# A graph network in two layers: the scan of layer 1 into SBUF, register loads of layer 2 in other places, and more columns fetched on chip

## The chip, the core and the metric

The kernel runs on one core of a Trainium2 chip. The core has five engines with a queue each: TensorE (PE in the profile, its weight loads PEld), VectorE (DVE), ScalarE (ACT), GpSimd (POOL) and SyncE (SP). They run side by side and meet at semaphores. Each queue is worked off in its order; some of its instructions, register loads for example, are done by the queue itself (DVEq and ACTq in the profile) and not by the engine behind it. The metric is device time in microseconds (us) of one execution, lower is better. Before the change it is 3579.78 us (median of 3 runs, 3579.74 to 3582.63).

## The reference

12500 nodes with 128 features and 200000 edges, sorted by destination (`dst`):

```python
h = maximum(layernorm(x), 0)
w = edge_weight / maximum(segment_sum(edge_weight, dst), EPS)[dst]
feat = relu(h @ W_pool + b_pool)
neigh = segment_max(feat[src] * w[:, None], dst)          # layer 1: a maximum per node
rst = h @ W1_self + neigh @ W1_neigh + b1
h = relu(rst / maximum(norm(rst), EPS))
neigh2 = segment_sum(h[src] * w[:, None], dst) / maximum(deg, 1)   # layer 2: a mean per node
out = x + relu(h @ W2_self + neigh2 @ W2_neigh + b2)
```

## The kernel before

Edges are worked in groups of 512, 391 groups, each of four chunks of 128 edges. A preparation computes `feat` and writes it to HBM (`feat_d`); then layer 1 runs over the groups, and layer 2 over them again. The order on each queue is the order in which the program is written out (a manual schedule), so a turn `i` of a loop issues different stages of several groups.

**Gathers and columns.** The rows `feat[src]` (layer 1) and `h[src]` (layer 2) of a chunk come by one indirect DMA from POOL (`gather`, line 520), 128 rows at a time, into a ring of buffers. Both tables also lie in SBUF with nodes as columns (`one_way`, `other_way`). For some groups one chunk is therefore not gathered: the class `Columns` copies its 128 columns out of the table, and PE turns them round. There are two such streams. Stream 0 runs on DVE and takes chunk 1: `two_by_two` (line 792) copies two columns by one instruction, 64 for a chunk. Stream 1 runs on ACT and takes chunk 3 in layer 1 and chunk 2 in layer 2: `one_by_one` copies one column by one instruction (line 780), 128 for a chunk. Which groups are taken is `first + int(n * every)`; `every` is 6 and 5.5 in layer 1, 3 and 3.5 in layer 2.

A column's place is known only at run time: a list of 128 places is brought to SBUF (`load`, on SP), and `places_of` loads 16 of them into registers of the engine's queue with one register load (line 742). A fetch is a burst of 16 columns with the registers loaded before; eight bursts make a chunk, spread over the turns ahead of its use (`plan`). `ahead` issues the register load for the next burst. With `ahead_of` false (both streams of layer 2, ACT's of layer 1) it is issued directly behind each burst; with `ahead_of` true (DVE's of layer 1) it waits for the call of `ahead` behind the scan, except between two bursts of one turn.

**Layer 1, a turn.** POOL gathers for group i. ACT scales the four chunks by the edge weights into `gs` (line 1027, two buffers). PE transposes `gs` into PSUM, `pm` (line 1032). DVE runs the segmented maximum along the edges with one scan, in place in PSUM (line 1047), with a mask `kt` that SP brings in from HBM for four groups at a time (`keep_rows`, `KEPT`). Then DVE copies the last column of the scan as `carry` (line 1066), copies every second column into `sc` (line 1070) and replaces some of these by their neighbours (`copy_predicated`, line 1073). PE transposes `sc` (line 1087), ACT copies the result to SBUF (`rows`, line 1042), and a product with a 0/1 matrix `sel` picks the last edge of each node. For column groups PE multiplies the columns by `W_pool`, and ACT applies the relu (`cut`, line 946). Besides, node tiles, and `side_step`s that prepare tables for layer 2, run in between. The first 16 groups take another way (rows of `x` gathered and multiplied).

**Layer 2, a turn.** DVE makes `hit` (line 1157) and from it the weighted places `s` (line 1160); between the two stands one burst of columns. PE multiplies the gathered rows by `s` into `pa` (line 1168). DVE adds the window of an earlier group to the sums (`window_add`, line 1171). The columns' chunks are turned round by PE into `flip` (`turned`, line 1143), and ACT copies them into the ring (`back`). At the end of the turn come the other bursts of both streams. Every fourth turn or so an output tile is finished (lines 902 and 903, DVE). The ring has eight buffers: POOL can gather into one when PE has used what it held.

## Time and profile before

| what | value |
|---|---|
| median of 3 runs | 3579.78 us |
| the profiled execution | 3579.99 us |
| its span in the trace | 3578.2 us |
| layer 1: first and last scan with a carry (line 1047) | 131.9 and 1843.1 us |
| layer 2: first and last gather of `h_d` into the ring | 1857.6 and 3546.9 us |
| gathers in layer 1 into `gt`, in layer 2 | 1192, 1318 |
| register loads of line 742: DVE, ACT | 1480, 1392 |
| granted TensorE clock, mean | 0.528 |

A row of a group of instructions reads: line, engine, operation, out<-in with shapes, count | busy us, mean ns of one | idle time of the engine in front of them and what ended it. Busy time is a union: instructions of one engine overlap, so busy divided by count can be less than the mean duration. Register loads, semaphores and the issue of DMAs are not counted as busy. In a row of waits stand the waiting engine and line, the one it waited for, then us in total, how often, and the longest. "issue" means that no other engine's event ended the wait.

### The profile page before, as it was taken

The numbers are of one execution on the slowest core, as the hardware profiler recorded it, in microseconds if no ns is written. First come the engines' busy times: TensorE is split into PE (matmuls) and PEld (weight loads), VectorE is DVE, ScalarE is ACT, GpSimd is POOL, SyncE is SP. The second block draws the span as 40 slices with busy tenths as digits, with TensorE's granted clock in tenths as the row PEclk, the third lists the DMA queues.
The fourth block names the chain that finished last, engine by engine and source line by source line (L and its number), as shares of the span: only waits on it lengthen the run. The fifth ranks groups of instructions, "written<-read, shape, count | busy, mean of one in ns | idle before, by whom it ended". The sixth has DMA issues, their size and how long they took to land.

```text
span 3578.2 us, 71950 instructions
## 1 busy us (share of the span) xinstructions
PE 2210.3 (62%) x9504; PEld 1929.0 (54%) x9504; DVE 3130.7 (87%) x16737; ACT 3087.4 (86%) x25633; POOL 2616.9 (73%) x2784
## 2 busy tenths in 40 slices
PE   7666666666766666566656666555655565555556
PEld 6455655565655555555545555544544454455445
DVE  7799999999999999998866888888888888888886
ACT  6689999999999998998948888888888888888885
POOL 6577777777777777777777777777777777777774
PEclk7665555555555555555555555555555555555555
DMA  6433222222222222222221122222222222222221
GB/s 222 130 95 95 87 88 83 87 87 87 91 88 87 86 88 86 86 87 82 86 78 54 54 66 69 62 60 63 58 60 58 61 57 61 60 59 57 60 62 46
DMA packets 132987, 280.13 MB, mean 78 GB/s; under 512 B 49446, under 2 KB 58764, under 8 KB 132494
## 3 DMA queue, kind: packets, MB, share of 16 engines
q0 software_dynamic: 88544, 181.42, 17.9%
q1 hardware_dynamic: 43214, 93.11, 7.5%
q14 instruction: 414, 3.39, 0.3%
q8 instruction: 79, 1.29, 0.2%
q10 hardware_dynamic: 736, 0.92, 0.1%
HBM read 253.41 MB, written 21.87 MB: 77 GB/s over the span
## 4 chain that ended last, share of the span: by engine, by line
DVE 42%; ACT 20%; issue 12%; DMA 7%; PE 7%; POOL 6%; DVEq 5%; ACTq 1%; POOLq 0%
DVE gt L792 22%; ACT gt L780 9%; POOL gt L520 6%; ACT gs L1027 6%; DVE pm L1047 4%; DVEq L742 4%; DVE picked L792 4%; DMA gt<-feat_d,srcT 4%; DMA gt<-h_d,srcT 3%; PE pa L1168 3%; DVE place L1157 2%; DVE sel L1059 2%; DVE way L1171 2%; PE pf L625 2%; DVE s L1160 1%
## 5 line engine op out<-in xcount | busy, mean ns | idle before, releaser
L780 ACT ACTIVATE gt<-way 128x1 f32 x21376 | 2123.3, 189 | 105.5 <-PE pa L1168 62.5
L520 POOL DMA_INDIRECT gt<-h_d,srcT x1318 | 1244.6, 944 | 446.3 <-issue 322.4
L520 POOL DMA_INDIRECT gt<-feat_d,srcT x1192 | 1126.7, 945 | 369.6 <-issue 271.5
L792 DVE SCALAR_TENSOR_TENSOR gt<-b,way 128x2 f32<-128x2 f32 x8000 | 1145.6, 214 | 64.9 <-issue 55.4
L1168 PE MATMUL pa<-s,gt 128*128 128x24 f32 x3102 | 736.7, 390 | 570.9 <-DVE s L1160 503.4
L1168 PEld LDWEIGHTS pa<-s,gt 128*128 128x128 f32 x3102 | 690.7, 328 | 608.5 <-DVE s L1160 533.4
L1032 PE MATMUL pm<-ident,gs 128*128 128x128 f32 x1499 | 398.9, 419 | 254.5 <-ACT gs L1027 230.6
L792 DVE SCALAR_TENSOR_TENSOR picked<-b,way 128x2 f32<-128x2 f32 x3840 | 542.0, 211 | 2.1 <-issue 1.8
L1047 DVE TENSOR_TENSOR_SCAN pm<-kt,carry,pm 128x512 f32<-128x512 bf16 x389 | 496.2, 1275 | 43.9 <-PE pm L1032 43.6
L1027 ACT ACTIVATE gs<-gt,ewT 128x128 f32<-128x128 f32 x1303 | 414.9, 390 | 73.2 <-DMA gt<-feat_d,srcT 59.4
L1096 PEld LDWEIGHTS pn<-sel,rows 128*128 128x128 f32 x1564 | 358.1, 316 | 164.7 <-ACT way L977 68.0
L1032 PEld LDWEIGHTS pm<-ident,gs 128*128 128x128 f32 x1499 | 288.2, 224 | 291.0 <-ACT gs L1027 266.6
L1096 PE MATMUL pn<-sel,rows 128*128 128x48 f32 x1564 | 360.4, 377 | 129.5 <-ACT way L977 53.5
L1059 DVE TENSOR_SCALAR sel<-cols,lastT,invT 128x48 f32<-128x48 f32 x782 | 244.1, 312 | 0.2 <-issue 0.2
L1087 PE MATMUL pr<-ident,sc 128*128 128x128 f32 x782 | 237.4, 405 | 3.5 <-DVE r_first L291 2.5
L1157 DVE TENSOR_TENSOR place<-place,locT 128x96 f32<-128x96 f32 x391 | 103.9, 266 | 108.9 <-DVE gt L792 80.5
L1160 DVE TENSOR_TENSOR s<-place,w2T 128x96 f32<-128x96 f32 x391 | 100.6, 257 | 82.0 <-DVE gt L792 67.4
L1087 PEld LDWEIGHTS pr<-ident,sc 128*128 128x128 f32 x782 | 165.5, 221 | 4.4 <-ACT gs L1027 3.8
L1073 DVE COPY_PREDICATED sc<-kt,pm 128x256 f32<-128x256 int16 x389 | 167.1, 429 | 0.0
L1070 DVE COPY sc<-pm 128x256 f32<-128x256 f32 x391 | 159.6, 408 | 4.0 <-PE pr L1087 3.9
L780 ACT ACTIVATE gt<-flip 128x128 f32<-128x128 f32 x108 | 29.6, 274 | 145.7 <-PE flip L1143 142.7
L1042 ACT ACTIVATE rows<-pr 128x256 f32<-128x256 f32 x392 | 141.8, 362 | 5.0 <-PE pn L1096 5.0
(303 smaller groups left out, 2774.9 us busy)
## 6 DMA issues: line engine op xcount, KB each, us to landing
kt<-keep_d SPq DMA_DIRECT2D x97, 512.0 KB
gt<-h_d,srcT POOLq DMA_INDIRECT x1318
gt<-feat_d,srcT POOLq DMA_INDIRECT x1192
feat_d<-fr SPq DMA_DIRECT2D x24, 256.0 KB
xr<-in_x SPq DMA_DIRECT2D x24, 256.0 KB
out<-o SPq DMA_DIRECT2D x24, 256.0 KB
h_d<-h SPq DMA_DIRECT2D x47, 128.0 KB
listed<-at_d SPq DMA_DIRECT2D x359, 0.5 KB
```

What stands on the lines that cost most here:

```text
L520: nc.gpsimd.indirect_dma_start(out=gt[:k, j, :], out_offset=None, in_=table_d[:, :], in_offset=bass.IndirectOffsetOnAxis(ap=srcT[:k, t, j, ...
L780: nc.scalar.activation(out, in_, AF.Copy, **scale)
L792: nc.vector.scalar_tensor_tensor(slot[:, r + e:r + e + 2], zero_high, columns_read[e], columns_read[e + 1].to_broadcast([P, 2]), op0=OP.su ...
L1027: nc.scalar.activation(gss[i][:k, j, :], gt[:k, j, :], AF.Copy, scale=ewT[:k, t, j, r:r + 1])
L1032: nc.tensor.transpose(pms[i - 1][:, j * P:j * P + k], gs[:k, j, :], ident[:k, :k])
L1047: nc.vector.tensor_tensor_scan(pm[:, :ne], kt[:, :ne], pm[:, :ne], carry, op0=OP.add, op1=OP.max)
L1059: nc.vector.tensor_scalar(part, cols[:k, 1, :], lastT[:k, t, j, r:r + 1], invT[:k, t, j, r:r + 1], op0=OP.is_equal, op1=OP.mult)
L1073: nc.vector.copy_predicated(sc[:, :ne // 2], new[:, :, 1], two[:, :, 0])
L1087: nc.tensor.transpose(prs[g][:k, j, :], sc[:, j * P:j * P + k], ident)
L1096: nc.tensor.matmul(pas[g], rows[:k, j, :], sel[:k, j, :], start=j == 0, stop=j == len(chunks) - 1)
L1157: nc.vector.tensor_tensor(hit, iota, locT[:, t, :, r:r + 1].to_broadcast([P, Q, CW]), OP.is_equal)
L1168: nc.tensor.matmul(pas[g][:, SHIFT[j]:SHIFT[j] + CW], gt[:k, j, :], s[:k, j, :], start=False, stop=j == 0)
```

## The change

- **Layer 1, scan.** The scan writes into the `gs` buffer of its group, in SBUF, in place of PSUM; `gs` has four buffers in place of two. The copy of every second column into `sc` is gone for all but the first 16 groups: `copy_predicated` works in place on every second column, and PE transposes those. `carry` is copied from SBUF. In the first 16 turns one product stands earlier.
- **Layer 1, mask.** It comes for three groups at a time, and the load is issued at the end of the turn.
- **Layer 1, columns.** `every` is 5 and 5.25.
- **Layer 2, register loads.** `ahead_of` is `None`: nothing is loaded directly behind a burst of DVE's. `ahead` is called behind `hit`, behind `s` and behind the window addition; a second burst stands ahead of the window addition; ACT's bursts stand around `back`, with `ahead` behind each of the later ones; `back` stands ahead of `turned`.
- **Layer 2, columns.** `every` is 2.85 and 3.3.

```diff
-KEPT = 4
+KEPT = 3
...
         def fetch(self, g, r):
+            if self.pending:
+                self.ahead()
             if (g, r) not in self.held:
                 self.places_of(g, r)
...
                     self.pending = g2, r2
-                    if not self.ahead_of or turn == self.order[now][2]:
+                    if self.ahead_of is False or self.ahead_of and turn == self.order[now][2]:
                         self.ahead()
...
+        def fetch_rest(self, i):
+            for step, g, r in self.plan.get(i, ()):
+                if step == self.fetch:
+                    step(g, r)
+                    self.ahead()
...
-                (0, mybir.EngineType.DVE, two_by_two, 1, 6, FIRST + 16),
-                (1, mybir.EngineType.Activation, one_by_one, 3, 5.5, FIRST + 12)):
+                (0, mybir.EngineType.DVE, two_by_two, 1, 5, FIRST + 16),
+                (1, mybir.EngineType.Activation, one_by_one, 3, 5.25, FIRST + 12)):
...
-            if i % KEPT == 0 and i and i + 2 < NG:
-                keep_rows(i + 2, keep_tile())
             if FIRST <= i < NG:
                 gts[i] = gather(buffer(i, True), feat_d, i, besides=bycol)
...
-                gss[i] = wk.tile([P, G], F32, name="gs", bufs=2).rearrange("p (q d) -> p q d", d=D)
+                gss[i] = wk.tile([P, G], F32, name="gs", bufs=4).rearrange("p (q d) -> p q d", d=D)
...
-                gs = gss.pop(i - 1)
+                gs = gss[i - 1]
...
-                nc.vector.tensor_tensor_scan(pm[:, :ne], kt[:, :ne], pm[:, :ne], carry,
+                most = gss.pop(g).rearrange("p q d -> p (q d)") if g >= FIRST else pm
+                nc.vector.tensor_tensor_scan(most[:, :ne], kt[:, :ne], pm[:, :ne], carry,
                                              op0=OP.add, op1=OP.max)
...
-                    nc.vector.tensor_copy(carry, pm[:, ne - 1:ne])
-                sc = scs[g] = wk.tile([P, G // 2], F32, name="sc", bufs=2)
-                two = pm[:, :ne].rearrange("p (c two) -> p c two", two=2)
-                new = kt[:, :ne].bitcast(I16).rearrange("p (c two) -> p c two", two=2)
-                nc.vector.tensor_copy(sc[:, :ne // 2], two[:, :, 1])
-            pick()
-            if g is not None:
-                nc.vector.copy_predicated(sc[:, :ne // 2], new[:, :, 1], two[:, :, 0])
+                    nc.vector.tensor_copy(carry, most[:, ne - 1:ne])
...
+            if g is not None:
+                two = most[:, :ne].rearrange("p (c two) -> p c two", two=2)
+                new = kt[:, :ne].bitcast(I16).rearrange("p (c two) -> p c two", two=2)
+                scs[g] = two[:, :, 1]
+                if g < FIRST:
+                    scs[g] = wk.tile([P, G], F32, name="gs", bufs=4)[:, :ne // 2]
+                    nc.vector.tensor_copy(scs[g], two[:, :, 1])
+            pick()
+            if g is not None:
+                nc.vector.copy_predicated(scs[g], new[:, :, 1], two[:, :, 0])
...
+            if i % KEPT == 0 and i and i + 2 < NG:
+                keep_rows(i + 2, keep_tile())
...
-                (0, mybir.EngineType.DVE, two_by_two, 1, 3, 17),
-                (1, mybir.EngineType.Activation, one_by_one, 2, 3.5, 12)):
+                (0, mybir.EngineType.DVE, two_by_two, 1, 2.85, 17),
+                (1, mybir.EngineType.Activation, one_by_one, 2, 3.3, 12)):
...
-            bycol.append(Columns(engine, copy, False, other_way, 1, lists_of(k), slot,
+            bycol.append(Columns(engine, copy, None, other_way, 1, lists_of(k), slot,
...
             nc.vector.tensor_tensor(hit, iota, locT[:, t, :, r:r + 1].to_broadcast([P, Q, CW]), OP.is_equal)
             if between:
+                bycol[0].ahead()
                 between()
...
                 weighted_places(i, lambda: bycol[0].fetch_one(i))
+                bycol[0].ahead()
...
+            by_two, by_one = bycol
+            by_two.fetch_one(i)
             g = i - 2
             if EARLY <= g < NG:
                 window_add(g, window_at(mybir.EngineType.DVE, g))
+            by_two.ahead()
+            by_two.turn(i, by_two.fetch)
+            by_one.fetch_one(i)
+            for c in bycol:
+                c.turn(i, c.back)
             for c in bycol:
                 c.turn(i, c.turned)
-                c.turn(i, c.back)
-            for c in bycol:
-                c.turn(i, c.fetch)
+            by_one.ahead()
+            by_one.fetch_rest(i)
```

More of the change, by code (lines that the diff above doesn't have):

```diff
@@ L1013, in gnn_kernel @@
                 if i + 1 < FIRST:
-                    weight_rows(i + 1, wk.tile([P, G], F32, name="gs", bufs=2))
+                    weight_rows(i + 1, wk.tile([P, G], F32, name="gs", bufs=4))
                     raw_columns(pn, i + 1)
```

## The prediction

> **What bounds the kernel now.** I read the first page, then the busy times by stretch, then each engine's waits inside a stretch, and last the instructions in order of time where the waits named no other engine.
>
> ```profile
> span 3578.2 us, 71950 instructions
> PE 2210.3 (62%) x9504; PEld 1929.0 (54%) x9504; DVE 3130.7 (87%) x16737; ACT 3087.4 (86%) x25633; POOL 2616.9 (73%) x2784
> DVE 42%; ACT 20%; issue 12%; DMA 7%; PE 7%; POOL 6%; DVEq 5%; ACTq 1%; POOLq 0%
> ...
> core 0: us, PE busy (x) PEld busy (x) DVE busy (x) ACT busy (x) POOL busy (x), PEclk, DMA share, GB/s
> 200.00:1100.00 900.00, 585.83 (x2631) 523.49 (x2631) 882.01 (x3741) 859.41 (x6338) 675.55 (x716) 0.54 0.29 88
> 1100.00:1800.00 700.00, 438.36 (x1934) 388.93 (x1932) 652.40 (x2848) 639.50 (x4756) 529.58 (x560) 0.53 0.28 86
> 2600.00:3400.00 800.00, 456.99 (x1923) 397.65 (x1923) 662.67 (x4505) 681.34 (x6719) 578.92 (x614) 0.50 0.21 59
> ```
>
> The page alone says "DVE and ACT, both nearly full". The stretches say more. From 200 to 1800 us (layer 1) DVE is 98% and then 93% busy, ACT 95% and 91%, and POOL issues a gather every 1.25 us (700 / 560). From 2600 to 3400 us (layer 2) no engine is full: DVE 83%, ACT 85%, POOL 72% with a gather only every 1.30 us (800 / 614). So in layer 2 something that is not counted as busy sets the pace.
>
> In layer 1 ACT's waits tell who leads. First row 200 to 1100 us, second 1100 to 1845, third 1700 to 1845 alone (time in total, times, longest):
>
> ```profile
> ACT gt L780 <- issue: 9.8, 24, 1.1
> ...
> ACT gs L1027 <- DMA gt<-feat_d,srcT: 59.1, 38, 4.4
> ...
> ACT gs L1027 <- DMA gt<-feat_d,srcT: 24.3, 12, 4.2
> ```
>
> Until 1100 us ACT does not wait for a gather at all; its longest entry is 9.8 us. After that it waits 59.1 us for them. The gathers start far ahead, the consumers catch up, and the end of layer 1 is set by POOL's rate.
>
> In layer 2, 2600 to 3400 us, the waits of DVE, POOL and PE are:
>
> ```profile
> DVE place L1157 <- DVE gt L792: 39.1, 135, 0.7
> DVE s L1160 <- DVE gt L792: 34.2, 148, 0.6
> DVE gt L792 <- issue: 28.3, 109, 1.0
> DVE place L1157 <- issue: 13.5, 43, 0.7
> ...
> DVE way L1171 <- PE pa L1168: 5.2, 10, 0.5
> ...
> POOL gt L520 <- PE pa L1168: 31.0, 31, 2.1
> POOL gt L520 <- PE pa L1166: 21.0, 32, 2.5
> ...
> PE pa L1168 <- DVE s L1160: 283.8, 133, 4.1
> ```
>
> Read from below: PE waits 284 us for DVE's `s`, POOL waits 52 us for PE to free a buffer of the ring, and DVE waits for nobody but itself (5.2 us for PE). DVE stands at the head, with holes of its own. What fills the holes is the register loads of line 742. The fence has them and the turns' first instruction, line 1157, in the same 800 us (count, then minimum/median/maximum ns, first and last start), and below them DVE's instructions in order of time (start, us):
>
> ```profile
> L742 DVEq TENSOR_LOAD <-listed x484: 1093/1096/1510, 2599.4 to 3399.0; - x162
> ...
> L1157 DVE TENSOR_TENSOR place<-place,locT x181: 265/266/267, 2602.7 to 3397.0; 128x96 f32<-128x96 f32 x181
> ...
> 2907.49 0.27 DVE L1157 TENSOR_TENSOR place<-place,locT 128x96 f32<-128x96 f32 x1 [0.23 <-DVE gt L792]
> 2907.66 1.12 DVE L792 SCALAR_TENSOR_TENSOR gt<-b,way 128x2 f32<-128x2 f32 x8
> 2909.03 0.26 DVE L1160 TENSOR_TENSOR s<-place,w2T 128x96 f32<-128x96 f32 x1 [0.25 <-DVE gt L792]
> 2909.21 0.20 DVE L1171 TENSOR_TENSOR way<-pa,way 128x48 f32 x1
> 2909.32 1.13 DVE L792 SCALAR_TENSOR_TENSOR gt<-b,way 128x2 f32<-128x2 f32 x8
> 2910.66 1.14 DVE L792 SCALAR_TENSOR_TENSOR gt<-b,way 128x2 f32<-128x2 f32 x8 [0.21 <-issue]
> 2912.10 0.27 DVE L1157 TENSOR_TENSOR place<-place,locT 128x96 f32<-128x96 f32 x1 [0.30 <-DVE gt L792]
> ```
>
> 484 loads of 1.096 us are 530 of the 800 us. They run on DVE's queue (DVEq), and nothing behind one is handed to the engine while it runs: `s` does not read the loaded registers, yet it stands 0.25 us behind the last copy. The rest, 270 us, spread over 4505 engine instructions is 60 ns each, little for issuing them. So **DVE's queue, not DVE, is full in layer 2**: load, issue, load, issue. A burst (one load and its eight two-column copies) costs 2912.10 − 2910.66 = **1.44 us**, although its copies keep the engine for 1.14.
>
> **Layer 2, part by part.** The steps 3 to 2.85 and 3.5 to 3.3 over groups 17 to 389 and 12 to 389 give 131 columns on DVE for 125 and 115 on ACT for 108. POOL loses 13 gathers, which earns nothing while POOL waits for DVE. DVE gains 6 × 8 = 48 bursts: 48 × 1.44 = **+69 us**. The nearest other prices are 1.65 us (800 / 484, as if all of the stage grew with the bursts), +79 us, and 1.10 us (the load alone), +53 us. I take 1.44 because it is a burst with nothing else in it.
>
> The moved loads. Before, a load follows its burst at once; after, it stands behind `hit`, behind `s` and behind the window addition, three places in a turn. Their number and length stay, and each still blocks what is behind it: `s`, the additions, the next copies, and behind `s` PE's products. A queue that never gets ahead of its engine gains nothing from another order. One thing shortens: in turns with an output tile, line 902 came behind `s` in the engine and now starts on an idle one. `s` holds the engine 0.17 us (2909.03 to 2909.21), so 98 tiles can win between 0 and 17 us; I take **−6**, a third, since `s` must still be issued. The fetch by `fetch_rest`, and `back` ahead of `turned`, concern ACT and PE. With 181 groups in 800 us a turn is 4.42 us, and ACT works 681 / 181 = 3.76 us of it; the 7 columns of 128 copies add some 0.22, against a DVE turn of about 4.6. That cover holds; ACT would have to grow by 0.6 us per group before it decides.
>
> **Layer 1, part by part.** The prices, from the groups of instructions (count, busy us, mean ns, idle time before them), and in the last two rows the first and last start of the scans and of the gathers:
>
> ```profile
> L780 ACT ACTIVATE gt<-way 128x1 f32 x21376 | 2123.3, 189 | 105.5 <-PE pa L1168 62.5
> L792 DVE SCALAR_TENSOR_TENSOR picked<-b,way 128x2 f32<-128x2 f32 x3840 | 542.0, 211 | 2.1 <-issue 1.8
> L1047 DVE TENSOR_TENSOR_SCAN pm<-kt,carry,pm 128x512 f32<-128x512 bf16 x389 | 496.2, 1275 | 43.9 <-PE pm L1032 43.6
> L1070 DVE COPY sc<-pm 128x256 f32<-128x256 f32 x391 | 159.6, 408 | 4.0 <-PE pr L1087 3.9
> ...
> L1073 DVE COPY_PREDICATED sc<-kt,pm 128x256 f32<-128x256 int16 x389 | 167.1, 429 | 0.0
> L1087 PE MATMUL pr<-ident,sc 128*128 128x128 f32 x782 | 237.4, 405 | 3.5 <-DVE r_first L291 2.5
> ...
> L1042 ACT ACTIVATE rows<-pr 128x256 f32<-128x256 f32 x392 | 141.8, 362 | 5.0 <-PE pn L1096 5.0
> ...
> L946 ACT ACTIVATE gt<-pn,b 128x128 f32<-128x128 f32 x52 | 18.6, 357 | 0.5 <-PE pn L943 0.5
> ...
> L414 DVE TENSOR_TENSOR_SCAN r_f<-r_goes,r_first,pq 128x512 f32<-128x512 bf16 x4 | 5.1, 1273 | 0.2 <-ACT pq L281 0.2
> ...
> L1047 DVE TENSOR_TENSOR_SCAN pm<-kt,carry,pm x389: 889/1276/1289, 131.9 to 1843.1; 128x512 f32<-128x512 bf16 x194, 128x320 f32<-128x320 bf16 x1
> ...
> L520 POOL DMA_INDIRECT gt<-feat_d,srcT x1192: 903/944/1378, 140.9 to 1837.1; - x199
> ```
>
> - Columns: 72 for 60 on DVE, 69 for 66 on ACT, 15 gathers fewer: 15 × 1.25 = **−18.8 us** of POOL.
> - DVE: the copy of line 1070 goes for 375 of 391 groups, −153 us; 12 columns of 542.0 / 60 = 9.03 us come, +108 us. Their loads stay behind the 1.28 us scan or eight copies; the idle time in front of these copies is 2.1 us in all now. DVE gets 45 us lighter, in a stage where it was 95% busy.
> - The scan writes SBUF: line 414 does that in 1273 ns, line 1047 writes PSUM in 1275. Nothing.
> - The predicated copy in place, all in SBUF, has no row. Between half and double of 429 ns it is −80 or +160 us of DVE; I take no change, by the scan, whose time does not care where it writes. Double would use up DVE's slack.
> - The carry from SBUF: one column, as now. PE transposes every second column of the scan: no row; if twice 405 ns, it is 0.8 us per group on a PE that is 35% idle there.
> - ACT: 3 columns × 128 × 99.3 ns = 38 us and some 15 more `cut`s at up to 0.36, **+43 us**. If all of it is on the consumers' path, it comes off their 59.1 us of waiting for gathers: they could end 59.1 − 43 = 16 us sooner. So I take **−16** for layer 1, between −18.8 and +8 (if the 24.3 us of them after 1700 can't be used).
> - `gs` in four buffers: ACT's scaling now waits until PE has transposed the scan of four groups before. ACT's row copy (line 1042) waited for that same transpose already, right behind it: at most its 5 us.
> - Keep rows by threes, at the turn's end: 130 loads for 98 on SP, each waiting for the predicated copy of the same turn, with list loads and stores of `h` behind it. The scan waits only for PE today (43.6 us in all), never for its mask; it keeps three turns of notice, at (1843.1 − 131.9) / 388 = 4.4 us each 13 us. Nothing.
> - In the first 16 turns three DVE operations change places; none comes or goes.
>
> **The sum**, against the profiled execution's own 3579.99 us (the median of the runs is 3579.78): 3580 − 16 + 69 − 6 = **3627 us**.
>
> **Rivals.**
> 1. *The moved loads hide* (the other side). If a load behind a longer instruction found the engine still occupied, DVE's holes would close; it needs 83% of its time. From then POOL decides:
>
> ```profile
> L520 POOL DMA_INDIRECT gt<-h_d,srcT x1318: 902/944/1147, 1857.6 to 3546.9; - x189
> ```
>
> These 1318 gathers took 1689 us; 1305 at 1.25 us take 1631, so layer 2 wins 58 us: 3580 − 16 − 58 = **3506 us**. The point where it decides: a turn of 4.42 us less its 2.67 bursts leaves 0.58 us; POOL's turn becomes 3.35 gathers × 1.25 = 4.18; so (4.18 − 0.58) / 2.81 = 1.28 us per burst. For it: in layer 1 the loads hide. Against it: there the engine has scan, copies and selections to do; here the load and its issue are longer than all the engine does. Chance 0.08. [...]
> 2. *Half hidden*: layer 2's 48 bursts are paid by closing half of DVE's holes: 3580 − 16 = **3564** up to 3590. Chance 0.07.
> 3. *ACT becomes the bound in layer 1*: +8 in place of −16: **3651 us**. For it: ACT at 95%. Against: the 59 us. Chance 0.10.
> 4. *Gathers held up by the predicated copy*: its mask and data both come from SBUF now. If each of 375 held POOL for 0.43 us, it were +160 us: **3787**. Against: the two-column copies of line 792 read two SBUF tensors all through layer 2, and the gathers beside them still take 944 ns. Chance 0.02. [...]
>
> **Chances and range.** The forecast (3605 to 3645 by the prices above) has 0.73. A measurement tells about 0.2%, 7 us, from no change. Faster: rival 1 and half of rival 2, 0.11. Same: 0.03. Slower: 0.86. Down to 3598 and up to 3654 takes in rival 3 and leaves out rivals 1, 4 and most of 2.
>
> **What would show it.** Layer 2: DVE's loads still 1.10 us each, 1048 in place of 1000; two bursts still 1.44 us apart; DVE's busy share no higher than 83 to 84%; a turn near 4.6 us; POOL waiting longer for PE. Layer 1: the last gather of `feat_d` some 16 us sooner than 1837.1, ACT above 95%. I am wrong if two bursts follow each other in under 1.3 us in layer 2, if POOL there no longer waits for PE, or if the last scan starts after 1843.1.

## The result, and the profile after

The changed kernel takes **3633.41 us** (median of 4 runs, 3632.71 to 3635.18) against 3580.95 for the kernel before (median of 4): a ratio of 1.0146 (95% interval 1.0132 to 1.016). The forecast was 3627. Its profiled execution took 3633.13 us, 53.1 more than the one before (3579.99). The page of the changed kernel, its head and its chain:

```profile
span 3631.3 us, 74688 instructions
PE 2238.5 (62%) x9562; PEld 1928.9 (53%) x9562; DVE 3242.0 (89%) x17514; ACT 3215.7 (89%) x26941; POOL 2618.1 (72%) x2756
DVE 35%; issue 7%; DVEq 5%; ACT 1%; PE 1%; POOL 1%; DMA 0%; ACTq 0%; POOLq 0%
```

The shares of this chain add up to 50% only: it can be followed back no further than 1783 us, so it shows layer 2 and almost nothing of layer 1, and it can't be set beside the 42% and 20% of the page of before, which cover the whole span. Where the time went is read off the first and last starts of the gathers (line 520, after):

```profile
L520 POOL DMA_INDIRECT gt<-h_d,srcT x1305: 904/945/1150, 1878.9 to 3602.9; - x187
L520 POOL DMA_INDIRECT gt<-feat_d,srcT x1179: 904/945/1390, 140.2 to 1858.5; - x197
```

| stretch | before | after | difference | forecast |
|---|---|---|---|---|
| layer 1, up to the last gather of `feat_d` | 1837.1 | 1858.5 | +21.4 | −16 |
| from there to the first gather of `h_d` | 20.5 | 20.4 | −0.1 | 0 |
| layer 2, first to last gather of `h_d` | 1689.3 | 1724.0 | +34.7 | +63 |
| from there to the end of the span | 31.3 | 28.4 | −2.9 | 0 |

The total came out 6 us from the forecast because two errors of opposite sign, +37 and −28, nearly cancel (the stretch at the end gives −3 more). That the number is close is luck. The busy times by stretch after (us, then PE, PEld, DVE, ACT, POOL):

```profile
200.00:1100.00 900.00, 578.15 (x2574) 507.01 (x2573) 885.19 (x3809) 857.68 (x6366) 667.82 (x692) 0.54 0.31 85
1100.00:1800.00 700.00, 443.71 (x1962) 387.03 (x1962) 688.13 (x3074) 662.63 (x4972) 532.06 (x552) 0.55 0.32 86
2600.00:3400.00 800.00, 453.69 (x1890) 391.57 (x1890) 676.79 (x4619) 707.64 (x7004) 561.86 (x595) 0.50 0.22 57
```

**Layer 1.** DVE is 98.3% busy from 200 to 1800 us (885.19 + 688.13 of 1600); before it was 95.9% (882.01 + 652.40). The pages' rows of the gathers, before and after, and the lines' own rows of the scan and the predicated copy after (count, minimum/median/maximum ns, first and last start), say why:

```profile
L520 POOL DMA_INDIRECT gt<-feat_d,srcT x1192 | 1126.7, 945 | 369.6 <-issue 271.5
```

```profile
L520 POOL DMA_INDIRECT gt<-feat_d,srcT x1179 | 1137.6, 965 | 378.8 <-issue 299.2
```

```profile
L1054 DVE TENSOR_TENSOR_SCAN gs<-kt,carry,pm x375: 880/1268/1281, 199.5 to 1864.6; 128x512 f32<-128x512 bf16 x187, 128x320 f32<-128x320 bf16 x1
...
L1086 DVE COPY_PREDICATED gs<-kt,gs x375: 515/720/745, 201.2 to 1865.8; 128x256 f32<-128x256 int16 x187, 128x160 f32<-128x160 int16 x1
```

The scan takes 1268 ns in SBUF, as long as in PSUM. The predicated copy takes **720 ns in place of 429**: 375 × 0.291 = +109 us of DVE. The twelve columns cost 642.8 − 542.0 = 101 us by the page's rows of DVE's column copies, a little less than the 108 forecast. So DVE did not lose 45 us of work, it gained −153 + 109 + 101 = +57; its whole busy time up to the last gather of `feat_d` went from 1720.0 to 1780.8 us, +61. And a gather of `feat_d` takes 965 ns on the mean, 945 before. ACT's wait for gathers from 1100 to 1850 us shows what the first of the two does:

```profile
ACT gs L1033 <- DMA gt<-feat_d,srcT: 4.3, 3, 2.4
```

The consumers wait 4.3 us for gathers where they waited 59.1 before: they catch up with POOL only at the very end, since DVE has 27 of the 1600 us left idle. But POOL is no less full. Its waits that ACT ended, so that a buffer came free, from 200 to 1800 us before and then from 200 to 1100 us after, and below them its usual pauses from 1100 to 1850 us after:

```profile
POOL gt L520 <- ACT rows L1042: 8.4, 7, 4.6
```

```profile
POOL gt L520 <- ACT rows L1048: 20.8, 4, 18.6
...
POOL gt L520 <- issue: 146.6, 481, 0.3
```

After one stop of 18.6 us, between 500 and 700 us, POOL makes only its constant pause of 0.3 us up to the last gather. So POOL's account gives the time of that gather. By the list of instructions, from the first gather of `feat_d` into the ring to the last: 15 gathers fewer (two of them into buffers of other names) −18.8, longer gathers +26, longer stops +15 (21 us in place of 6, beyond the constant pauses), together +22, against the 21.4 measured. The first of the three is the forecast's. The second comes from the scan's part, as experiment 5 shows. The third fits the full DVE: POOL had run ahead until no buffer was free. So DVE and POOL end layer 1 nearly together, and neither is the bound alone.

**Layer 2.** The register loads, the turns' first instruction and the waits of POOL and PE from 2600 to 3400 us:

```profile
L742 DVEq TENSOR_LOAD <-listed x500: 1093/1097/1629, 2600.1 to 3399.8; - x167
...
L1169 DVE TENSOR_TENSOR place<-place,locT x177: 247/256/267, 2602.3 to 3396.9; 128x96 f32<-128x96 f32 x177
...
POOL gt L520 <- PE pa L1181: 61.4, 61, 5.3
POOL gt L520 <- PE pa L1179: 14.8, 15, 4.5
...
PE pa L1181 <- DVE s L1173: 276.5, 122, 6.4
```

The picture is the one of before. The loads still last 1.10 us, PE still waits some 280 us for `s`, POOL waits for PE even more (76 us, 52 before), and DVE is 84.6% busy. Yet 500 loads fit into 800 us where 484 did, and a turn takes 800 / 177 = 4.52 us for the 4.6 expected. Something in the new order saves more than the 6 us that it was given.

What it is shows in the trace's list of instructions: the time from the end of one register load to the start of the next, by what DVE's queue issues between them (2600 to 3400 us, medians):

```
between two loads of DVE                             before   after
8 copies                                             0.348    0.348
8 copies and place (or s)                            0.385    0.385
8 copies, window addition (before: and s)            0.532    0.495
the same with an output tile (902/903; 910/911)      1.010    0.590
```

A burst with nothing else is as dear as it was: 0.348 + 1.097 = 1.44 us. But an **output tile** cost the queue 1.010 − 0.532 = 0.478 us before and costs 0.590 − 0.495 = 0.095 after. For 98 tiles that is 98 × 0.383 = **−37.5 us**, and 69 − 37.5 = +31.5, about the 34.7 measured. (The two rows leave out tiles with another register load in between. After the change a third of the rest has a semaphore instruction besides and 0.64 to 0.66 us; the tile shown below is one of them. With these the median is 0.604, and the 98 tiles are worth 36 us.) In order of time, before and then after (DVE's instructions, start, us):

```profile
2666.71 0.26 DVE L1160 TENSOR_TENSOR s<-place,w2T 128x96 f32<-128x96 f32 x1 [0.16 <-issue]
2666.89 0.28 DVE L902 TENSOR_TENSOR o<-pn,b 128x128 f32<-128x128 f32 x1
2667.20 0.29 DVE L903 SCALAR_TENSOR_TENSOR o<-o,xr 128x128 f32<-128x128 f32 x1
2667.41 0.20 DVE L1171 TENSOR_TENSOR way<-pa,way 128x48 f32 x1
2667.53 1.13 DVE L792 SCALAR_TENSOR_TENSOR gt<-b,way 128x2 f32<-128x2 f32 x8
```

```profile
2629.07 0.25 DVE L1173 TENSOR_TENSOR s<-place,w2T 128x96 f32<-128x96 f32 x1
2629.49 0.29 DVE L910 TENSOR_TENSOR o<-pn,b 128x128 f32<-128x128 f32 x1 [0.17 <-issue]
2629.82 0.29 DVE L911 SCALAR_TENSOR_TENSOR o<-o,xr 128x128 f32<-128x128 f32 x1
2630.02 1.14 DVE L800 SCALAR_TENSOR_TENSOR gt<-b,way 128x2 f32<-128x2 f32 x8
2631.09 0.20 DVE L1184 TENSOR_TENSOR way<-pa,way 128x48 f32 x1
```

Line 903 needs the result of 902 and starts 0.034 us after its end (2667.168). Behind it stands, before, the window addition, whose first piece is register arithmetic that the queue does itself (0.069 us on DVEq). It began at 2667.216 us, just after 903 had been released (2667.202); only then could the eight copies be issued, and only behind them the next load (2667.649, 1.03 us after the end of the last one at 2666.623). After the change eight copies stand there, with no register arithmetic among them. They are issued while 911 waits: the window addition's register arithmetic, which stands behind all eight, begins at 2629.893, 0.08 us after the release of 911 (2629.815), where eight copies alone take 0.348 between two loads, and the next load starts at 2630.055, 0.66 us after the end of the last one (2629.399).

### The profile page after: what moved, and what is told of

Same layout as the page of the kernel before. It is cut to its first block, busy times and chain, and to the rows that moved or that the text cites. A ratio compares the mean times of both kernels' runs of the same rounds, so it can differ in the third digit from the quotient of the medians.

```text
span 3631.3 us, 74688 instructions
## 1 busy us (share of the span) xinstructions
PE 2238.5 (62%) x9562; PEld 1928.9 (53%) x9562; DVE 3242.0 (89%) x17514; ACT 3215.7 (89%) x26941; POOL 2618.1 (72%) x2756
## 4 chain that ended last, share of the span: by engine, by line
DVE 35%; issue 7%; DVEq 5%; ACT 1%; PE 1%; POOL 1%; DMA 0%; ACTq 0%; POOLq 0%
DVE gt L800 28%; DVEq L742 4%; DVE place L1169 2%; DVE s L1173 2%; DVE way L1184 1%; POOL gt L520 1%; ACT gt L788 1%; DVE o L910 1%; PE pa L1181 1%; DVE gs L1054 0%; DVE o L911 0%; DVE picked L800 0%; DMA gt<-h_d,srcT 0%; ACT gs L1033 0%; DVEq L839 0%
## 5 line engine op out<-in xcount | busy, mean ns | idle before, releaser
L788 ACT ACTIVATE gt<-way 128x1 f32 x22528 | 2240.6, 189 | 193.5 <-PE pa L1181 121.4
L800 DVE SCALAR_TENSOR_TENSOR gt<-b,way 128x2 f32<-128x2 f32 x8384 | 1206.6, 215 | 201.5 <-issue 178.7
L800 DVE SCALAR_TENSOR_TENSOR picked<-b,way 128x2 f32<-128x2 f32 x4608 | 642.8, 211 | 2.1 <-issue 1.7
L1054 DVE TENSOR_TENSOR_SCAN gs<-kt,carry,pm 128x512 f32<-128x512 bf16 x375 | 475.2, 1267 | 16.9 <-PE pm L1038 7.0
L1086 DVE COPY_PREDICATED gs<-kt,gs 128x256 f32<-128x256 int16 x375 | 270.0, 720 | 0.6
L1097 PE MATMUL pr<-ident,gs 128*128 128x128 f32 x782 | 238.7, 406 | 4.6 <-DVE b L808 1.9
L1097 PEld LDWEIGHTS pr<-ident,gs 128*128 128x128 f32 x782 | 165.2, 225 | 11.9 <-issue 5.4
L851 PE MATMUL pn<-w_2n,way 128*128 128x128 f32 x192 | 77.7, 508 | 111.6 <-DVE way L1184 111.2
L520 POOL DMA_INDIRECT w2T<-feat_d,srcT x94 | 90.4, 962 | 52.8 <-issue 22.9
L851 PEld LDWEIGHTS pn<-w_2n,way 128*128 128x128 f32 x192 | 52.3, 321 | 134.2 <-DVE way L1184 133.9
```

The source lines that it names most:

```text
L520: nc.gpsimd.indirect_dma_start(out=gt[:k, j, :], out_offset=None, in_=table_d[:, :], in_offset=bass.IndirectOffsetOnAxis(ap=srcT[:k, t, j, ...
L788: nc.scalar.activation(out, in_, AF.Copy, **scale)
L800: nc.vector.scalar_tensor_tensor(slot[:, r + e:r + e + 2], zero_high, columns_read[e], columns_read[e + 1].to_broadcast([P, 2]), op0=OP.su ...
L1054: nc.vector.tensor_tensor_scan(most[:, :ne], kt[:, :ne], pm[:, :ne], carry, op0=OP.add, op1=OP.max)
L1086: nc.vector.copy_predicated(scs[g], new[:, :, 1], two[:, :, 0])
L1097: nc.tensor.transpose(prs[g][:k, j, :], sc[:, j * P:j * P + k], ident)
```

## The experiments

Twelve runs were made, of eight kernels. One thing has to be known first: they ran on chips of two kinds. On one kind the kernel before takes 3579 to 3581 us, on the other 5039 to 5159, and the kernels with an edit that met it took 5026 to 5160. The largest difference in those traces is in ACT's waits. They are shown from 300 to 4800 us for a kernel (`columns_layer2`, below) with only the columns of layer 2 changed:

```profile
ACT gt L780 <- issue: 1236.0, 2081, 1.9
ACT gs L1027 <- issue: 43.0, 95, 1.1
```

ACT stands still 1236 us ahead of its one-column copies, waiting for nothing that the trace shows; the same row of before had 33 us. One copy lasts 187 ns on both, and most follow each other at 93 ns on both, but on these chips there are stretches in which two copies of ACT start some 0.70 us apart, or 1.30 to 1.40. DVE's two-column copies have more of such idle time too, 257 us for 55. PE waits for ACT above all (774.9 us ahead of its products of layer 2 for these columns in `loads_moved`), so there ACT sets the pace, and a time from there says little of the change. Instructions' durations and the usual gaps of DVE's queue can still be read there. What slows ACT stays open.

**1. Each part alone.** Four kernels, each the kernel before with one part of the change:

`loads_moved`: the new order of layer 2, columns as before.

```diff
-            bycol.append(Columns(engine, copy, False, other_way, 1, lists_of(k), slot,
+            bycol.append(Columns(engine, copy, None, other_way, 1, lists_of(k), slot,
...
+                bycol[0].ahead()
...
+            by_two.fetch_one(i)
...
+            by_two.ahead()
+            by_two.turn(i, by_two.fetch)
```

> The kernel before with the turn of layer 2 in the changed order (register loads behind hit, s and the window addition, a burst ahead of the window addition, back ahead of turned), columns as before in both layers. Theory from the two traces: an output tile costs DVE's queue 0.38 us less in this order, 98 tiles, so 37 us are won and the bursts still cost 1.44 us: 3580 - 37 = 3543 us, DVE's turn in layer 2 from 4.42 to about 4.32 us. Rival, the prediction's own term: the order is worth 6 us, 3574 us. Second rival: the loads hide behind longer instructions, the turn falls to POOL's 4.23 us, about 3515 us.

`columns_layer2`: only 2.85 and 3.3, with `back` ahead of `turned`.

```diff
-                (0, mybir.EngineType.DVE, two_by_two, 1, 3, 17),
-                (1, mybir.EngineType.Activation, one_by_one, 2, 3.5, 12)):
+                (0, mybir.EngineType.DVE, two_by_two, 1, 2.85, 17),
+                (1, mybir.EngineType.Activation, one_by_one, 2, 3.3, 12)):
```

> The kernel before with the columns of layer 2 alone at each 2.85th and 3.3rd group; back stands ahead of turned, since two columns can now be two turns apart; the register loads stay directly behind their bursts. Theory: 48 bursts more at 1.44 us on a queue that is full, 3580 + 69 = 3649 us, DVE's turn in layer 2 about 4.6 us, POOL waiting longer for PE. Rival: fewer gathers shorten layer 2 by 13 x 1.25 = 16 us, 3564 us.

`columns_layer1`: only 5 and 5.25.

```diff
-                (0, mybir.EngineType.DVE, two_by_two, 1, 6, FIRST + 16),
-                (1, mybir.EngineType.Activation, one_by_one, 3, 5.5, FIRST + 12)):
+                (0, mybir.EngineType.DVE, two_by_two, 1, 5, FIRST + 16),
+                (1, mybir.EngineType.Activation, one_by_one, 3, 5.25, FIRST + 12)):
```

> The kernel before with the columns of layer 1 alone at each 5th and 5.25th group; the scan stays in PSUM. Theory: DVE is full in layer 1 until the consumers catch up, so 12 columns of 9.03 us weigh on it (108 us) and 15 gathers fewer (19 us) win nothing: the consumers had 59 us of waiting to give, layer 1 ends some 40 us later, 3620 us, DVE 98% busy to the end. Rival: POOL sets the end of layer 1, 3561 us.

`scan_sbuf`: the scan into SBUF with four buffers of `gs`, the predicated copy in place and the mask by threes; columns and layer 2 as before.

```diff
-                nc.vector.tensor_tensor_scan(pm[:, :ne], kt[:, :ne], pm[:, :ne], carry,
+                most = gss.pop(g).rearrange("p q d -> p (q d)") if g >= FIRST else pm
+                nc.vector.tensor_tensor_scan(most[:, :ne], kt[:, :ne], pm[:, :ne], carry,
...
-                nc.vector.copy_predicated(sc[:, :ne // 2], new[:, :, 1], two[:, :, 0])
+                nc.vector.copy_predicated(scs[g], new[:, :, 1], two[:, :, 0])
```

> The kernel before with the scan of layer 1 into SBUF, the predicated copy in place, four gs buffers and the mask by threes; columns of both layers and the order of layer 2 as before. Theory: the copy that is gone (408 ns) less the dearer predicated copy (720 for 429 ns) makes DVE 117 ns per group lighter, but gathers that start inside a predicated copy take some 200 ns more, about 26 us over layer 1, and POOL sets the end of layer 1: it ends 15 to 25 us later, 3595 to 3605 us. Rival: the DVE work decides and layer 1 is no longer than before or shorter, 3580 us or less.

All four met a chip on which before takes 5158.64 us:

| kernel | us | ratio, 95% interval |
|---|---|---|
| `loads_moved` | 5095.81 | 0.9878 (0.9857 to 0.9899) |
| `columns_layer2` | 5153.81 | 0.9991 (0.9981 to 1.0001) |
| `columns_layer1` | 5160.43 | 1.0 (0.9986 to 1.0014) |
| `scan_sbuf` | 5142.36 | 0.9978 (0.9966 to 0.999) |

None of the expected times can be compared. That the columns cost nothing there fits a DVE with room behind ACT (57% busy from 2600 to 3400 us in `columns_layer2`, 458.12 of 800); why the order gains 63 us there is not shown. Two readings hold all the same. In `scan_sbuf` the predicated copy takes 723 ns (median), so its price belongs to the scan's part alone. And the gathers grow with that part alone; the page's rows of `scan_sbuf`, and then of `columns_layer1`:

```profile
L520 POOL DMA_INDIRECT gt<-feat_d,srcT x1192 | 1149.3, 964 | 920.6 <-ACT rows L1048 414.5
```

```profile
L520 POOL DMA_INDIRECT gt<-feat_d,srcT x1179 | 1112.8, 944 | 961.5 <-ACT rows L1042 403.0
```

**2. What makes the predicated copy dear.** `probe` puts 60 predicated copies of 128x256 ahead of the kernel before, twelve of each of five forms. They work on values that the kernel does not use.

```diff
+    half = probe_c[:, :G // 2]
+    for _ in range(12):
+        nc.vector.copy_predicated(half, when, even_p)
+        nc.vector.copy_predicated(half, when, even_s)
+        nc.vector.copy_predicated(odd_s, when, even_s)
+        nc.vector.copy_predicated(odd_s, when, even_p)
+        nc.vector.copy_predicated(odd_p, when, even_p)
```

> The kernel before with 60 predicated copies of 128x256 put ahead of everything, twelve of each of five forms, on tiles that nothing else uses then (they add some 35 us): destination contiguous in SBUF and data in PSUM (the form before, about 429 ns); destination contiguous and data in SBUF; destination each second column and data in SBUF (the form after, about 720 ns); destination each second column in SBUF and data in PSUM; all but the mask in PSUM. If the dearer copy comes from two SBUF inputs, mask and data, the second and the third form take about 720 ns and the fourth about 430. If it comes from the destination with a step, the third and the fourth take 720 and the second 430.

The five lines in the order of the diff (`_s` is SBUF, `_p` PSUM, `half` a dense tile in SBUF):

```profile
L506 DVE COPY_PREDICATED way<-way,pq x12: 440/440/441, 5.9 to 35.1; 128x256 f32<-128x256 int16 x12
...
L507 DVE COPY_PREDICATED way<-way x12: 445/446/446, 6.4 to 35.6; 128x256 f32<-128x256 int16 x12
...
L508 DVE COPY_PREDICATED way<-way x12: 718/719/720, 6.8 to 35.9; 128x256 f32<-128x256 int16 x12
...
L509 DVE COPY_PREDICATED way<-way,pq x12: 721/722/723, 7.5 to 36.7; 128x256 f32<-128x256 int16 x12
...
L510 DVE COPY_PREDICATED pq<-way,pq x12: 517/520/521, 8.0 to 37.2; 128x256 f32<-128x256 int16 x12
```

Data in SBUF or in PSUM makes no difference (446 to 440; 719 to 722). A destination of **every second column** does: 719 in SBUF where a dense one takes 446, and 520 in PSUM. It is the place written to, not two operands in SBUF, that costs 0.28 us here. (The time of the kernel, 5080.04 against 5046.2, is one of the other chips.)

**3. The order alone, on a chip where before takes 3579.44 us.** `loads_moved_2` is `loads_moved` again. `order_balanced` is the same with the columns of layer 2 each 3.1th group on DVE and each 3.3rd on ACT:

```diff
-                (0, mybir.EngineType.DVE, two_by_two, 1, 3, 17),
-                (1, mybir.EngineType.Activation, one_by_one, 2, 3.5, 12)):
+                (0, mybir.EngineType.DVE, two_by_two, 1, 3.1, 17),
+                (1, mybir.EngineType.Activation, one_by_one, 2, 3.3, 12)):
```

> The kernel of loads_moved once more, for a chip with the queues of the profile of before. Theory: 3580 - 37 = 3543 us. Rivals: 3574 us (the prediction's term), 3515 us (loads hidden).

> The kernel before with the changed order of layer 2 and its columns at each 3.1th (DVE) and 3.3th (ACT) group; layer 1 untouched. Where the queues run as in the profile of before (3580 us): a turn of DVE's queue is 0.45 us and 2.58 bursts of 1.44, 4.17 us, POOL's is 3.37 gathers of 1.25, 4.22 us, so layer 2 goes from 4.42 to about 4.25 us a turn, and the time to about 3515 us, 65 us under before. If the order is worth only the prediction's 6 us, DVE's turn is 4.27 and the time about 3530. On a chip where ACT's queue is the slow one, as in the last runs (before 5046 to 5159 us), the seven further ACT columns cost: then slower than the order alone, 0.99 of before or more.

`loads_moved_2` took **3544.16** us and `order_balanced` **3515.92** (one run each). Layer 1 is as before in both (last gather of `feat_d` at 1836.1 and 1836.7 us), so nearly the whole gain is layer 2's: the new order by itself is worth 35.3 us, against the 37.5 worked out from the tiles and the 6 of the prediction. The gaps of `loads_moved_2` are those of after: 0.590 with a tile, 0.495 without. ACT's bursts stand in other places too, but these gaps of DVE account for the whole gain.

```profile
L520 POOL DMA_INDIRECT gt<-h_d,srcT x1318: 903/944/1152, 1856.6 to 3512.4; - x189
```

This row of `loads_moved_2` prices the columns of layer 2 as well, since in layer 2 it and the changed kernel differ in nothing but the columns. From the first to the last gather of `h_d` it takes 1655.8 us, 33.5 less than before; the changed kernel takes 1724.0. So the 48 bursts more, with 13 gathers fewer, cost **68.2 us**, 1.42 us a burst, where the prediction had 69.

The turns, loads and waits of POOL in layer 2 of `order_balanced`, 2600 to 3400 us:

```profile
L1165 DVE TENSOR_TENSOR place<-place,locT x190: 250/262/268, 2601.1 to 3395.6; 128x96 f32<-128x96 f32 x190
...
L742 DVEq TENSOR_LOAD <-listed x492: 1093/1097/1555, 2600.4 to 3399.8; - x164
...
POOL gt L520 <- PE pa L1177: 17.4, 57, 0.3
POOL gt L520 <- DMA gt<-h_d,srcT: 6.7, 22, 0.3
```

A turn takes 800 / 190 = 4.21 us. POOL's waits for PE are now 57 times 0.3 us, no longer than its own pause between two gathers (before, the longest were 2.1 and 2.5 us), and the trace has 641 gathers in the 800 us, one every 1.25: POOL is full. Fewer columns for DVE and more for ACT bring DVE's queue down to POOL's rate, and there the three meet. This version beats both kernels, by 63.5 us the one before.

**4. The parts again, and one burst.** `columns_layer2_2`, `columns_layer1_2` and `scan_sbuf_2` repeat kernels of (1). `burst_ahead` has a single line of the new order, a second burst ahead of the window addition, and so behind the output tile:

```diff
+            bycol[0].fetch_one(i)
             g = i - 2
             if EARLY <= g < NG:
                 window_add(g, window_at(mybir.EngineType.DVE, g))
```

> The kernel of columns_layer2 once more, for a chip with the queues of the profile of before. Theory: 48 bursts at 1.44 us on a full queue, 3580 + 69 = 3649 us; DVE's turn in layer 2 near 4.6 us. Rival: 13 gathers fewer, 3564 us.

> The kernel of columns_layer1 once more, for such a chip. Theory: DVE is full, 108 us of columns come on it, the consumers never catch up with the gathers, layer 1 ends some 40 us later: 3620 us. Rival: POOL sets the end of layer 1, 3561 us.

> The kernel of scan_sbuf once more, for such a chip. Theory: DVE gets some 44 us lighter (153 off, 109 on by the copy into each second column) and the consumers catch up sooner, but gathers that begin inside a predicated copy take 200 ns more, so POOL ends layer 1 15 to 25 us later: 3595 to 3605 us. Rival: the gathers' excess is hidden, 3580 us or less.

> The kernel before with one thing of the changed order alone: in layer 2 a second burst of DVE stands ahead of the window addition; register loads stay directly behind their bursts. Theory: an output tile costs the queue 0.48 us because the register arithmetic of the window addition waits for the tile's second operation, which waits for its first; eight copies in between hide most of that: 0.2 us remain, 98 x 0.28 = 27 us won, 3553 us. If the win needs the loads behind s, this stays at 3580; if all of it comes from the burst, 3543.

They met a chip on which before takes 5038.92 us: 5031.93, 5051.02, 5053.12 and 5025.94, one run each, and none of the expected times can be told from these. So no kernel with the columns alone was timed on a chip of the kind that the prediction was made for; what the columns cost there comes from differences between kernels, in (3) for layer 2 and in (5) for layer 1. Of `burst_ahead` DVE's gaps can be read: with an output tile, `s` and eight copies between two loads the median is 0.607 us, and 0.39 without the tile. A tile costs the queue 0.22 us there, as expected, where it cost 0.478 before and 0.095 after. The one burst behind the tile takes more than half of that cost away; that it does so in time, without the moved loads, is not shown.

**5. What the scan into SBUF does by itself.** `scan_and_order` is the changed kernel with layer 1's columns as before and DVE's columns of layer 2 as in `order_balanced`; against `order_balanced` only the scan's part is left.

```diff
-                (0, mybir.EngineType.DVE, two_by_two, 1, 5, FIRST + 16),
-                (1, mybir.EngineType.Activation, one_by_one, 3, 5.25, FIRST + 12)):
+                (0, mybir.EngineType.DVE, two_by_two, 1, 6, FIRST + 16),
+                (1, mybir.EngineType.Activation, one_by_one, 3, 5.5, FIRST + 12)):
...
-                (0, mybir.EngineType.DVE, two_by_two, 1, 2.85, 17),
+                (0, mybir.EngineType.DVE, two_by_two, 1, 3.1, 17),
```

> The changed kernel with the columns of layer 1 back at each 6th and 5.5th group and those of layer 2 at each 3.1th and 3.3th: the scan into SBUF with the predicated copy in place, and the changed order of layer 2. Where the queues run as in the profile of before, layer 2 is that of order_balanced (3516 us), and the difference to it is layer 1's scan alone. DVE's account: 153 us off, 109 us on, 44 us lighter, so the consumers catch up sooner and POOL's rate decides; if the gathers' excess beside the predicated copies then counts (some 20 ns a gather over 1374), layer 1 ends 20 to 28 us later than 1837, 3536 to 3544 us. If DVE's account alone decides, layer 1 ends where it did, 3516 us or a little less. On a chip with the slow ACT queue nothing of this shows.

It took **3541.04** us (median of 4, 3536.96 to 3544.8) against 3581.39: a ratio of 0.9886 (0.9869 to 0.9902), 25 us above `order_balanced`. All of that is layer 1: the last gather of `feat_d` starts at 1864.2 us, 27.5 later than in `order_balanced`. And DVE is not the cause. The busy times of `scan_and_order` by stretch, and ACT's waits from 1100 to 1850 us:

```profile
200.00:1100.00 900.00, 586.75 (x2625) 522.75 (x2624) 858.64 (x3512) 855.23 (x6300) 683.48 (x704) 0.53 0.29 87
1100.00:1800.00 700.00, 421.51 (x1870) 372.49 (x1869) 624.94 (x2637) 620.28 (x4607) 532.60 (x550) 0.54 0.28 85
...
ACT gs L1033 <- DMA gt<-feat_d,srcT: 55.0, 32, 4.0
```

DVE is down to 92.7% (1483.58 of 1600), and the consumers wait 55.0 us for gathers: POOL leads, as before the change, but it is slower. The page's rows of the gathers, of `scan_and_order` and of `order_balanced`:

```profile
L520 POOL DMA_INDIRECT gt<-feat_d,srcT x1192 | 1155.8, 970 | 365.3 <-issue 269.7
```

```profile
L520 POOL DMA_INDIRECT gt<-feat_d,srcT x1192 | 1125.8, 944 | 370.1 <-issue 304.7
```

970 − 944 = 26 ns on 1192 gathers are 31 us. The idle time ahead of them is the same, so the gathers themselves are longer. Not all are. In order of time, POOL and the predicated copies of `scan_and_order` (start, us):

```profile
843.08 0.94 POOL L520 DMA_INDIRECT gt<-feat_d,srcT  x1 [0.30 <-issue]
843.39 0.74 DVE L1086 COPY_PREDICATED gs<-kt,gs 128x256 f32<-128x256 int16 x1
...
847.84 0.73 DVE L1086 COPY_PREDICATED gs<-kt,gs 128x256 f32<-128x256 int16 x1
848.07 1.13 POOL L520 DMA_INDIRECT gt<-feat_d,srcT  x1 [0.30 <-issue]
```

A gather that starts 0.31 us ahead of the copy keeps its 0.94 us; one that starts 0.23 us behind it takes 1.13. By the list of instructions (200 to 1845 us), of the gathers that start 0 to 0.3 us after a predicated copy began, 110 of 110 are longer than 1.0 us in `scan_and_order` and 113 of 113 in the changed kernel; with the copy out of PSUM, in `order_balanced`, 1 of 79. The sooner behind the copy, the longer: 1.28 us within 0.1 us of its start, 1.16 within 0.2, 1.12 within 0.3. All but 4 of the 223 end 1.33 to 1.36 us after the copy's start wherever they began, 0.62 us after its end. From 0.4 us on nothing happens (0.94). Those that start less than 0.1 us *ahead* of the copy are held too, and longest: 10 of 10 in `scan_and_order` and 2 of 2 in the changed kernel, 1.36 to 1.43 us; from 0.15 us ahead on they are not. Three things are new in this copy at once: its data come from SBUF, it writes every second column, and it lasts 0.72 us. Which of them holds the gathers up was not tried.

The changed kernel differs from `scan_and_order` in layer 1 only by its columns, and its last gather of `feat_d` starts at 1858.5 us in place of 1864.2. So with the scan in SBUF the columns of layer 1 are worth −5.7 us, and the scan's part +27.5.

## Why the prediction was right or wrong

**The bound.** DVE's queue, not DVE, is full in layer 2 (84.6% busy in the changed kernel): right. More bursts cost time, and the order that relieves the queue (`loads_moved_2`) gives 35.3 us back with the same columns and gathers.

**48 bursts × 1.44 us.** Right: load 1.097 and gap 0.348 stay within a nanosecond, no two loads of layer 2 start less than 1.44 us apart, and the changed kernel's layer 2 is 68.2 us longer than that of `loads_moved_2`, from which it differs by the columns alone.

**The order, −6.** This step failed in size and in its reason: it is −35 (3579.44 to 3544.16). "A queue that never gets ahead of its engine gains nothing from another order" was wrong. An output tile did hold the queue, by a wait for the engine ahead of register arithmetic, and its 0.478 us could have been read from before's own trace: 1.010 against 0.532 between two loads. I looked at `s` ahead of line 902, not at what stood behind line 903.

**The predicated copy: "no change".** This step failed: 720 for 429 ns, inside the bounds of half and double, but at the dear end. I took the value by the scan, which takes as long into SBUF as into PSUM (1268 and 1276 ns); the scan's destination is dense, the copy's is every second column, and `probe` shows that this is what counts. The nearest row was the wrong one. With +109 us DVE got heavier by some 60 in place of lighter by 45.

**Layer 1, −16.** It came out +21.4, and two steps failed. The first is the price of a gather: by POOL's rate of 1.25 us 15 gathers fewer give −18.8, but the scan's part makes the gathers of layer 1 26 us longer, and alone it moves the last one by +27.5 (`scan_and_order`). The second is "they could end 16 us sooner", which supposed that DVE had room. Before, DVE had 65.6 us idle in the 1600 us; some 60 more nearly fill them. The 59.1 us of waiting for gathers, from which I took ACT's 43, were eaten by DVE, POOL stopped 18.6 us for want of a buffer, and the columns gave 5.7 us in place of 18.8. "Double would use up DVE's slack" named it; it stood under no rival.

**Rival 4, the gathers held up by the predicated copy.** I gave it 0.02, since the two-column copies leave the gathers at 944 ns. The hold-up is there, at a smaller price: about one gather in ten by some 0.2 us, 26 ns on the mean, 25 to 28 us in layer 1 when DVE has room (`scan_and_order`), not 375 × 0.43. In the changed kernel it is there in full (+26 us in POOL's account). How much of it would come back without the hold-up is not shown, since DVE is 98.3% busy there as well. The row that I set against this rival was true (two-column copies with two SBUF inputs last 0.21 us and leave the gathers' mean at 944), but it says nothing of an instruction of 0.72 us; that the length is what counts was not tried.

**Rivals 1 to 3.** Rival 1 (loads hide, POOL decides) did not happen in the changed kernel, but its end state was near: `order_balanced` reaches it, POOL full at 1.25 us per gather. Half hidden came nearest in layer 2 (+34.7), by another cause than the one named. ACT, rival 3, is not the bound in layer 1: it is 95.0% busy there (857.68 + 662.63 of 1600), DVE 98.3%.

**The signs.** Of the three things that would have made me wrong, the last scan came after 1843.1 (at 1864.6): layer 1's theory fell there. The other two did not occur: bursts keep their distance, and POOL still waits for PE.

## What to carry to other kernels

Where a queue, not its engine, is the bound, measure the gap between two of the queue's own instructions by what stands in between, and put plain engine instructions behind one that waits for its own engine. Here the output tile, whose second instruction does so, cost the queue 0.095 us with eight copies behind it and 0.478 with register arithmetic; a register load behind it (line 831, before) started 13 to 15 ns after its release, in 21 of 21 tiles. The price of a form that the trace does not show (here a stepped destination, 720 ns for 429) comes from a row with the same access, or from twelve of them ahead of the kernel, before anything else is built on it. And an engine with as little room as DVE here (65.6 of 1600 us) needs its own sum for every edit that may add to it, whichever engine the waits name now; so does the engine whose instructions run beside the one that is changed (here POOL, 26 ns a gather).

## What the runs showed of the hardware

- In `probe` a predicated copy of 128x256 fp32 takes 440 to 446 ns into a dense tile in SBUF, 719 to 722 into every second column there and, with its data in PSUM, 520 into every second column of PSUM. Into SBUF it takes as long with its data from SBUF as from PSUM (446 and 440, 719 and 722).
- A gather of GpSimd that starts up to 0.3 us after the predicated copy in place (data and mask in SBUF, every second column written there, 0.72 us) lasts over 1.0 us in place of 0.94 (223 of 223 in two kernels; all but 4 end 0.62 us after the copy's end), and so does one that starts less than 0.1 us ahead of it (12 of 12, 1.36 to 1.43 us).
- While line 903 (911 after the change) waits for 902 (910), register arithmetic behind it is not done until it is released: it begins 0.014 us after that in the tile shown of before. Eight copies in between are issued meanwhile: in the tile shown of after the arithmetic behind them begins 0.08 us after the release. The same two instructions cost the queue 0.478 or 0.095 us, by what follows them.
- The kernel before takes 3580 us on some chips and 5039 to 5159 on others. There, in `columns_layer2`, ACT stands still 1236 us ahead of its one-column copies (33 us on the first kind, `before`), in stretches in which two of them start some 0.70 or 1.30 to 1.40 us apart. Why is open.
